# The first layer of a two-layer macaron block, laid out as one ordered stage with its mixtures beside the scan

## The chip, the core and the metric

The kernel runs on one core of a Trainium2 chip, in one launch. The metric is the device time in microseconds of that core, the median of several executions. The engines are PE (matmul, with PEld for its weight loads), DVE (vector), ACT (scalar functions), POOL (GpSimd) and SP, which only issues DMAs here. [...]

## The reference

The input x is 4 batches of 1024 tokens of 128 channels, all in fp32. Two layers follow, each a mixture, an attention-like part and the same mixture again. Only the first layer is touched:

```python
x = x + 0.5 * _L0_ffn_ref(_layernorm(x, axis=-1), ...)
x = x + _L0_attn_ref(_layernorm(x, axis=-1), ...)
x = x + 0.5 * _L0_ffn_ref(_layernorm(x, axis=-1), ...)
```

`_L0_ffn_ref` is a mixture of experts. A router gives 8 logits per token, the two best experts are kept and their softmax weights are scaled to sum to 1. Each expert is `w2 @ square(relu(w1 @ x))`. A shared expert, twice as wide, is added for every token. `_L0_attn_ref` is a selective state-space scan:

```python
u, res = jnp.split(x @ W_in, 2, axis=-1)
u = silu(conv of 3 taps over u, with W_conv)
dt, Bm, Cm = jnp.split(u @ W_x, [8, 24], axis=-1)
delta = jax.nn.softplus(dt @ W_dt + b_dt)
deltaA = jnp.exp(jnp.einsum('bld,dn->bldn', delta, A))
deltaB_u = jnp.einsum('bld,bln->bldn', delta * u, Bm)
# for each token: h = deltaA * h + deltaB_u;  y = sum over n of h * C
y = (y + u * D_param) * jax.nn.silu(res)
return y @ W_out
```

There are 256 inner channels (`DI` = 2 blocks of 128, index c) and 16 states (`NS`, index n).

## The kernel before

x stays in SBUF for the whole kernel, as `x_sb`, with 128 tokens on the partitions and 32 token tiles, 8 for each batch. The first layer runs as three stages: `moe0` over all batches, `s6` over all batches, `moe0` again. Instructions are put in order by a scheduler within and across these stages, following data dependences.

**moe0** (L152). For each batch: `layernorm_t` (L98) computes the statistics on DVE (L83, L84, and Newton steps L93 to L95 for the reciprocal root), normalizes (L108, DVE) and transposes on PE to channels on partitions, `xnt`. `route` (L120) makes logits and ranks them on DVE (L127 to L146). Then, for each half of 512 tokens and each expert, `hidden` makes hp by one 128x512 matmul (L181), Relu on ACT (L183), and squares on POOL (L185, `r*r`). Four 128x128 matmuls give `op` (L214, or L195 for the shared expert), and DVE adds `op` times the token's weight to `x_sb` (L218, four 128x128 operations an expert; L202 for the shared one). Three PSUM banks serve hp and three serve op.

**s6** (L231). For each batch: normalization; the input projection (L264), a copy, three DVE operations for the convolution (L273, L277) and Silu; `xd` by W_x (L291); softplus in pieces on DVE and ACT (L308 to L323), giving `delta` and `du`. Then the states, for each half of 512 tokens and each n: `sel` matmuls broadcast the row of B and the row of C over 128 partitions, `bp` (L334) and `cp` (L336), in PSUM; ACT copies cp to `c_sb` (L338). For each c, ACT makes `da` (L341), DVE makes `db = du * bp` (L345), with bp read from PSUM, and scans (L347). In the first half POOL copies the last column for the second half (L356). POOL multiplies by C (L358, `hm`), and PE adds hm into `yp` over n by an identity matmul (L359). After the 16 n, DVE adds `u * D`, multiplies by Silu(res) (L364, L372), PE projects (L376), and DVE adds to `x_sb` (L384).

Layer 1 starts with `moe1`, whose normalization and routing of all 4 batches take 1291 to 1342 us in the trace; the rest of layer 1 (head attention, mostly) follows and is not changed.

Of the kernel before, what the change touches and what calls it, by code (L numbers as in the profile page):

```python
# [20 lines left out]
I32 = mybir.dt.int32  # L21
# [55 lines left out]

def ln_stats(nc, sb, x, mv, rstd):

    n = x.shape[1]  # L80
    for i in range(n):
        st = sb.tile([P, nc.vector.BN_STATS_DIM], F32, name="ln_st", bufs=4)
        nc.vector.bn_stats(st, x[:, i, :])  # L83
        nc.vector.bn_aggr(mv[:, i, :], st)  # L84

    a = sb.tile([P, n], F32, name="ln_a")
    nc.vector.tensor_scalar(a, mv[:, :, 1], EPS, None, op0=ALU.add)
    q = sb.tile([P, n], F32, name="ln_q")
    nc.vector.tensor_scalar(
        rstd.bitcast(I32), a.bitcast(I32), -0.5, RSQRT, op0=ALU.mult, op1=ALU.add  # L90
    )
    for _ in range(3):
        nc.vector.scalar_tensor_tensor(q, rstd, -0.5, rstd, op0=ALU.mult, op1=ALU.mult)  # L93
        nc.vector.tensor_tensor(q, q, a, op=ALU.mult)
        nc.vector.scalar_tensor_tensor(rstd, q, 1.5, rstd, op0=ALU.add, op1=ALU.mult)  # L95
# [24 lines left out]
def route(nc, k, sb, ps, xnt, w_router, ex, mask):  # L120


    lg = ps.tile([P, GT, E], F32, name="lg", tag="tr")
    for i in range(GT):
        nc.tensor.matmul(lg[:, i, :], xnt[:, ts(i, P)], w_router, start=True, stop=True)
    mx = sb.tile([P, GT], F32, name="rt_mx")
    nc.vector.tensor_reduce(mx, lg, AX.X, ALU.max)  # L127
    d = sb.tile([P, GT, E], F32, name="rt_d")
    nc.vector.tensor_tensor(d, lg, mx[:, :, None].to_broadcast([P, GT, E]), op=ALU.subtract)
    nc.scalar.activation(ex, d, AF.Exp)  # L130
# [5 lines left out]
    eq = sb.tile([P, GT, E, E], F32, name="rt_eq")  # L136
    nc.vector.tensor_tensor(eq, other, own, op=ALU.is_equal)
    nc.vector.tensor_tensor(
        eq, eq, k.tri[:, None, :, :].to_broadcast([P, GT, E, E]), op=ALU.mult
    )  # L140
    above = sb.tile([P, GT, E, E], F32, name="rt_above")
# [6 lines left out]

def moe0(tc, k):  # L152


    nc = tc.nc
    with (
        tc.tile_pool(name="m0", bufs=2) as sb,
        tc.tile_pool(name="m0_tr", bufs=2, space=PSUM) as ps_tr,
        tc.tile_pool(name="m0_h", bufs=3, space=PSUM) as ps_h,
        tc.tile_pool(name="m0_o", bufs=3, space=PSUM) as ps_o,  # L160
    ):
        for g in range(B):
            xnt = sb.tile([P, L], F32, name="xnt")
            layernorm_t(nc, k, sb, ps_tr, g, xnt)
            ex = sb.tile([P, GT, E], F32, name="ex")
            mask = sb.tile([P, GT, E], F32, name="mask")
            route(nc, k, sb, ps_tr, xnt, k.wr0, ex, mask)

            w = sb.tile([P, GT, E], F32, name="w")
            nc.vector.tensor_tensor(w, ex, mask, op=ALU.mult)  # L170
            tot = sb.tile([P, GT], F32, name="tot")
            nc.vector.tensor_reduce(tot, w, AX.X, ALU.add)
            nc.vector.reciprocal(tot, tot)
            nc.vector.scalar_tensor_tensor(
                w, w, 0.5, tot[:, :, None].to_broadcast([P, GT, E]), op0=ALU.mult, op1=ALU.mult
            )

            def hidden(w1, cols):

                hp = ps_h.tile([P, 512], F32, name="hp")  # L180
                nc.tensor.matmul(hp, w1, xnt[:, cols], start=True, stop=True)  # L181
                r = sb.tile([P, 512], F32, name="r", bufs=3)
                nc.scalar.activation(r, hp, AF.Relu)  # L183
                h = sb.tile([P, 512], F32, name="h", bufs=4)
                nc.gpsimd.tensor_tensor(h, r, r, op=ALU.mult)  # L185
                return h

            for half in range(2):
                cols = ts(half, 512)
                t0 = g * GT + half * 4  # L190
                hs = [hidden(k.ws1[:, ts(f, P)], cols) for f in range(FS)]
                op = ps_o.tile([P, 4, C], F32, name="op")
                for i in range(4):
                    for f in range(FS):
                        nc.tensor.matmul(  # L195
                            op[:, i, :],
                            hs[f][:, ts(i, P)],
                            k.ws2[:, f, :],
                            start=(f == 0),
                            stop=(f == FS - 1),  # L200
                        )
                nc.vector.scalar_tensor_tensor(  # L202
                    k.x_sb[:, t0 : t0 + 4, :],
                    op,
                    0.5,
                    k.x_sb[:, t0 : t0 + 4, :],
                    op0=ALU.mult,
                    op1=ALU.add,
                )
                for e in range(E):  # L210
                    h = hidden(k.w1_0[:, e, :], cols)
                    op = ps_o.tile([P, 4, C], F32, name="op")
                    for i in range(4):
                        nc.tensor.matmul(  # L214
                            op[:, i, :], h[:, ts(i, P)], k.w2_0[:, e, :], start=True, stop=True
                        )
                    for i in range(4):
                        nc.vector.scalar_tensor_tensor(  # L218
                            k.x_sb[:, t0 + i, :],
                            op[:, i, :],  # L220
                            w[:, half * 4 + i, e : e + 1],
                            k.x_sb[:, t0 + i, :],
                            op0=ALU.mult,
                            op1=ALU.add,
                        )
# [5 lines left out]
def s6(tc, k):  # L231

    nc = tc.nc
    HL = 512
    with (
        tc.tile_pool(name="s6_c", bufs=1) as cst,
        tc.tile_pool(name="s6_b", bufs=2) as sb,
        tc.tile_pool(name="s6_w", bufs=3) as wk,
        tc.tile_pool(name="s6_tr", bufs=2, space=PSUM) as ps_tr,
        tc.tile_pool(name="s6_bc", bufs=2, space=PSUM) as ps_bc,  # L240
        tc.tile_pool(name="s6_y", bufs=1, space=PSUM) as ps_y,
    ):

        NR = DTR + 2 * NS
        sel = cst.tile([NR, 2 * NS, P], F32, name="sel")
        nc.vector.tensor_copy(sel, k.ident[0:NR, DTR:NR, None].to_broadcast([NR, 2 * NS, P]))
# [4 lines left out]
        for b in range(B):  # L251
            xnt = sb.tile([P, L], F32, name="xnt", bufs=1)
            layernorm_t(nc, k, sb, ps_tr, b, xnt)


            u = sb.tile([P, DI, L], F32, name="u")
            res = sb.tile([P, DI, L], F32, name="res")
            for c in range(2 * DI):
                if c < DI:
                    up = sb.tile([P, L + 2], F32, name="up", bufs=1)  # L260
                    nc.gpsimd.memset(up[:, 0:2], 0.0)
                for half in range(2):
                    pin = ps_tr.tile([P, HL], F32, name="pin", tag="tr")
                    nc.tensor.matmul(  # L264
                        pin, k.w_in[:, ts(c, P)], xnt[:, ts(half, HL)], start=True, stop=True
                    )
                    if c < DI:
                        nc.scalar.copy(up[:, 2 + half * HL : 2 + (half + 1) * HL], pin)
                    else:
                        nc.scalar.activation(res[:, c - DI, ts(half, HL)], pin, AF.Silu)  # L270
                if c < DI:
                    cv = sb.tile([P, L], F32, name="cv", bufs=1)
                    nc.vector.tensor_scalar(  # L273
                        cv, up[:, 0:L], k.w_conv[:, c, 0:1], None, op0=ALU.mult
                    )
                    for j in (1, 2):
                        nc.vector.scalar_tensor_tensor(  # L277
                            cv,
                            up[:, j : j + L],
                            k.w_conv[:, c, j : j + 1],  # L280
                            cv,
                            op0=ALU.mult,
                            op1=ALU.add,
                        )
                    nc.scalar.activation(u[:, c, :], cv, AF.Silu)

            xd = sb.tile([NR, L], F32, name="xd")
            for half in range(2):
                pxd = ps_tr.tile([NR, HL], F32, name="pxd", tag="tr")
                for c in range(DI):  # L290
                    nc.tensor.matmul(  # L291
                        pxd,
                        k.w_x[:, c, :],
                        u[:, c, ts(half, HL)],
                        start=(c == 0),
                        stop=(c == DI - 1),
                    )
                nc.scalar.copy(xd[:, ts(half, HL)], pxd)

# [862 lines left out]
```

## Time and profile before

| | us |
|---|---|
| runs shown, median | 8650.8 |
| runs shown, range | 8642.8 to 8652.7 |
| profiled execution, its time | 8645.8 |
| profiled execution, span of the trace | 8644.0 |
| ... first mixtures, 0 to 197 | 197 |
| ... scans of 4 batches with their preparation, 197 to 1108 | 911 |
| ... second mixtures, 1108 to 1291 | 183 |
| ... layer 1, 1291 to the end | 7353 |

The span is the time between the first and the last instruction in the trace. A line of a group names the kernel's line, the engine, the operation, what it writes and reads, and how often. PE's granted clock is given as a share of full speed.

The page's rows of busy tenths, 40 slices of 216 us each, show the first layer as the first six:

```profile
DVE  6766676777777777777777777777777777777773
ACT  2333324999999999999999999999999999999993
POOL 3554440000000000000000000000000000000000
PEclk9777797999999999999999999999999999999996
```

POOL works in the first layer alone. From the seventh slice on ACT is full: that is layer 1.

### The profile page before, as it was taken

The page shows a single profiled execution, that of the slowest core. Times are in us where ns is not written, and L with a number is a line of the kernel's source. Part 1 is how long each engine was busy: PE and PEld are TensorE (multiplying, and loading weights), DVE is VectorE, ACT ScalarE, POOL GpSimd, SP SyncE. Part 2 cuts the span into 40 slices and gives each one's busy share as a digit, 9 for nine tenths or more (in the row PEclk, how much of TensorE's full clock was granted, in tenths as well). Part 3 has the DMA queues.
Part 4 walks back from the last instruction along what each step waited for, and adds up shares of the span by engine and source line. Part 5 has one row for each costly group of instructions (what it writes and reads, how often), then busy time and mean ns, then how long its engine had stood idle before and what let it go on. Part 6 is the DMA issues. An engine that isn't in the chain of part 4 may idle for free. (4 is left out here: it accounts for less than half of the span.)

```text
span 8644.0 us, 174023 instructions
## 1 busy us (share of the span) xinstructions
PE 7278.9 (84%) x76602; PEld 3189.2 (37%) x76602; DVE 6580.4 (76%) x14818; ACT 7447.6 (86%) x1746; POOL 621.7 (7%) x642
## 2 busy tenths in 40 slices
PE   8888886888888888888888988888888888888885
PEld 5222253333333333333333433333334333333333
DVE  6766676777777777777777777777777777777773
ACT  2333324999999999999999999999999999999993
POOL 3554440000000000000000000000000000000000
PEclk9777797999999999999999999999999999999996
DMA  0000000000000000000000000000000000000000
GB/s 19 0 0 0 0 6 4 2 1 2 1 1 2 1 1 2 2 1 1 2 1 1 1 1 1 2 1 2 1 1 1 1 1 1 1 1 2 1 1 16
DMA packets 14660, 20.06 MB, mean 2 GB/s; under 512 B 3242, under 2 KB 12978, under 8 KB 13876
## 3 DMA queue, kind: packets, MB, share of 16 engines
q8 instruction: 611, 10.01, 0.5%
q1 hardware_dynamic: 9572, 6.01, 0.2%
q10 hardware_dynamic: 4304, 2.62, 0.1%
q14 instruction: 173, 1.42, 0.1%
HBM read 6.53 MB, written 2.10 MB: 1 GB/s over the span
## 5 line engine op out<-in xcount | busy, mean ns | idle before, releaser
L870 ACT ACTIVATE p_w<-xs,cc 128x7936 f32<-128x7936 f32 x1024 | 6971.4, 6898 | 92.3 <-PE o L880 73.9
L880 PE MATMUL o<-p_w,vt 128*9 128x256 f32 x63488 | 3829.5, 387 | 700.7 <-ACT p_w L870 695.2
L880 PEld LDWEIGHTS o<-p_w,vt 128*9 128x9 f32 x63488 | 1792.2, 92 | 2590.9 <-ACT p_w L870 1065.2
L789 DVE SCALAR_TENSOR_TENSOR x_p<-x_p,x_r 128x256 f32<-128x256 f32 x3072 | 1306.3, 425 | 105.4
L888 DVE COPY os<-o 128x256 f32<-128x256 f32 x1024 | 431.9, 422 | 580.4 <-PE o L880 579.5
L765 DVE COPY xs<-s 128x1024 f32<-128x1024 f32 x512 | 626.5, 1224 | 203.6 <-PE s L729 202.2
L743 DVE TENSOR_REDUCE nm<-s 128x1 f32<-128x1024 f32 x512 | 625.6, 1222 | 200.0 <-PE s L729 199.7
L880 PE MATMUL o<-p_w,vtop 128*9 128x256 f32 x2048 | 626.0, 388 | 9.8 <-DVE vtop L803 9.8
L906 PE MATMUL pt<-ident,os 128*128 128x128 f32 x2048 | 455.0, 304 | 168.7 <-DVE os L888 162.7
L729 PE MATMUL s<-kp,qp 32*128 32x512 f32 x2048 | 587.0, 650 | 0.7 <-DVE nm L743 0.7
L729 PE MATMUL s<-qp,kp 32*128 32x512 f32 x2048 | 583.1, 646 | 0.0
L906 PEld LDWEIGHTS pt<-ident,os 128*128 128x128 f32 x2048 | 208.2, 142 | 926.5 <-DVE os L888 789.0
L790 DVE SCALAR_TENSOR_TENSOR p_w<-x_p,x_e 128x256 f32<-128x256 f32 x1024 | 435.8, 426 | 109.4 <-DVE x_p L789 3.2
L359 PE MATMUL yp<-hm,ident 128*128 128x512 f32 x512 | 387.7, 878 | 105.5 <-POOL hm L358 103.9
L699 POOL COPY wp_q<-c_wq 128x32 f32<-128x32 f32 x32 | 6.9, 215 | 6151.4 <-PE pq L708 6151.4
L341 ACT ACTIVATE da<-delta,neg_a 128x512 f32<-128x512 f32 x256 | 182.7, 721 | 305.2 <-DVE hst L347 304.7
L787 DVE SCALAR_TENSOR_TENSOR x_p<-x_r 128x256 f32<-128x256 f32 x1024 | 429.1, 419 | 0.1
L781 DVE TENSOR_TENSOR x_r<-x_r,x_p 128x256 f32<-128x256 f32 x1024 | 428.5, 419 | 0.0
L358 POOL TENSOR_TENSOR hm<-hst,c_sb 128x512 f32<-128x512 f32 x256 | 369.9, 1457 | 172.6 <-ACT c_sb L338 119.7
L774 DVE TENSOR_SCALAR x_r<-xs,cc 128x256 f32<-128x256 f32 x1024 | 353.1, 345 | 1.0
L778 DVE TENSOR_SCALAR x_e<-x_p 128x256 int32<-128x256 f32 x1024 | 301.6, 295 | 35.0
L776 DVE TENSOR_SCALAR x_p<-x_r 128x256 f32<-128x256 f32 x1024 | 301.5, 294 | 35.0
(189 smaller groups left out, 4816.6 us busy)
## 6 DMA issues: line engine op xcount, KB each, us to landing
x_sb<-in_L_attn_x_dram ACTq DMA_DIRECT2D x4, 512.0 KB
c_w<-in_L_ffn_w_dram SPq DMA_DIRECT2D x4, 512.0 KB
out_dram<-x_sb SPq DMA_DIRECT2D x4, 512.0 KB
c_w<-in_L_ffn_w_stack_dram SPq DMA_DIRECT2D x1, 512.0 KB
c_w<-in_L_ffn_w_stack_dram ACTq DMA_DIRECT2D x1, 512.0 KB
c_ws<-in_L_ffn_ws_dram SPq DMA_DIRECT2D x2, 128.0 KB
c_w_in<-in_L_attn_W_in_dram SPq DMA_DIRECT2D x1, 256.0 KB
c_w_out<-in_L_attn_W_out_dram SPq DMA_DIRECT2D x1, 128.0 KB
```

The source lines that it names most:

```text
L359: nc.tensor.matmul(yp[c], k.ident, hm, start=(n == 0), stop=(n == NS - 1))
L729: nc.tensor.matmul(s[:, ts(half, 512)], a[row, ts(i, P)], c[row, ts(half, 512)], start=True, stop=True,)
L743: nc.vector.tensor_reduce(nm[:, i, 0:1], score(j, qp[n], i, kp[n]), AX.X, ALU.max, negate=True)
L765: nc.vector.tensor_copy(xs[u][:, i, :], score(j, kp[n], i, qp[n]))
L781: nc.vector.tensor_tensor(r, r, p, op=ALU.subtract)
L787: nc.vector.scalar_tensor_tensor(p, r, EXP2[4], r, op0=ALU.add, op1=ALU.mult)
L789: nc.vector.scalar_tensor_tensor(p, p, c, r, op0=ALU.add, op1=ALU.mult)
L790: nc.vector.scalar_tensor_tensor(p_w[g][:, 0, 0:SOFT], p, EXP2[0], e.bitcast(F32), op0=ALU.add, op1=ALU.mult,)
L870: nc.scalar.activation(p_w[g].rearrange("p a b -> p (a b)")[:, SOFT:], xs[u].rearrange("p a b -> p (a b)")[:, SOFT:], AF.Exp, scale=cc[:, ...
L880: nc.tensor.matmul(o[32 * r : 32 * r + D + 1, 0:QW], vtop[u] if soft else vts[b % 2][:, i, h, :], p_w[g][:, i, ts(r, QW)], start=(i == 0), ...
L888: nc.vector.tensor_copy(os, o[:, 0:QW])
L906: nc.tensor.transpose(pt[:, wl % 2 * 2 + c, :], os[:, ts(c, P)], k.ident)
```

## The change

`moe0` and `s6` are replaced by one function, `layer0`, whose instructions keep the order in which they are written, on all five queues. The pieces are generators, which are drawn in turn. The order:

- `route_rows(0)`, `route_rows(1)`, both halves of `experts(0)`, `prepare(0)`, `softplus(0)`.
- For each batch b: 18 steps of `states(b)`. After each step up to three pieces (two from step 10 on) of `beside(b)` are issued, and, once the batch's first mixture is through, one piece of `prepare(b + 1)`. `beside(b)` holds the first mixture of batch b + 1 and, from b = 1 on, the second mixture of batch b - 1. For the last batch only the latter.
- Then `close(b)` and `softplus(b + 1)` in turn, with two pieces of what is left of `beside(b)` after each, then the rest.
- At the end the second mixture of the last batch.

What is computed otherwise than before:

- The states run over 1024 columns at once, so that the scan needs no carried column (L356 goes). Rows of B and C are written to DRAM once a batch, and each n is read back into all 128 partitions by DMA, as `bc` (1 MB). `du` is thus multiplied by a tile in SBUF. POOL's product is written over the scan's result.
- The mixture's weights go into the square: the root of each token's weight (by an exponential of half the logit, and the reciprocal root of the sum) is written to DRAM and read back over 128 partitions as `m_w`; POOL multiplies Relu's result by it, ACT squares, and all ten products are added up in PSUM. DVE adds once for each half.
- The normalization's scaling goes from DVE to ACT. The convolution is put into the weights: `w_cv` is W_in times each tap, and three matmuls over shifted columns add up. W_conv is loaded over all partitions.
- PSUM: four banks for y, and one each for hp, op, the mixtures' transposes and the scan's small tiles.

The core of the diff:

```diff
+        tc.tile_pool(name="l0_y", bufs=1, space=PSUM) as ps_y,
+        tc.tile_pool(name="l0_t", bufs=1, space=PSUM) as ps_t,
+        tc.tile_pool(name="l0_r", bufs=1, space=PSUM) as ps_r,
+        tc.tile_pool(name="l0_h", bufs=1, space=PSUM) as ps_h,
+        tc.tile_pool(name="l0_o", bufs=1, space=PSUM) as ps_o,
+        tc.manual_schedule(engines=engines),
     ):
         neg_a = cst.tile([P, DI, NS], F32, name="neg_a")
         nc.scalar.activation(neg_a, k.a_log, AF.Exp)
         nc.vector.tensor_scalar(neg_a, neg_a, -1.0, None, op0=ALU.mult)
...
+        def route_rows(m):
+
+            m_x[m] = mb.tile([P, L], F32, name="m_x")
+            yield from normed(mb, ps_r, m % B, m_x[m])
+            lg = ps_r.tile([P, GT, E], F32, name="lg", tag="tr")
...
+            best_two(nc, mb, lg, d, mask, k.tri)
+
+            ex = mb.tile([P, GT, E], F32, name="ex")
+            nc.scalar.activation(ex, d, AF.Exp, scale=0.5)
+            yield
...
+                nc.sync.dma_start(out=m_rows[m][:, ts(half, HL)], in_=row)
+            yield
...
+        def experts(m, half, after):
...
+            for i in range(n + 2):
+                if i == 1:
+                    weights(m, half, 1)
+                if i == 7 and after:
+                    weights(*after, 0)
+                if i >= 2:
+                    j = i - 2
...
+                        nc.tensor.matmul(
+                            op[:, a, :],
+                            h[j][:, ts(a, P)],
+                            w2,
...
+                if i < n:
...
+                    nc.tensor.matmul(hp, w1, m_x[m][:, ts(half, HL)], start=True, stop=True)
+                    r[i] = mb.tile([P, HL], F32, name="r", bufs=3)
+                    nc.scalar.activation(
+                        r[i], hp, AF.Relu, scale=ROOT if i < FS else 1.0
+                    )
+                if 1 <= i <= n:
+                    j = i - 1
+                    if j >= FS:
+                        e = j - FS
+                        nc.gpsimd.tensor_tensor(
+                            r[j], r[j], m_w[m, half, e // 4][:, e % 4, :], op=ALU.mult
+                        )
+                    h[j] = mb.tile([P, HL], F32, name="h", bufs=3)
+                    nc.scalar.activation(h[j], r[j], AF.Square)
+                yield
+            nc.vector.tensor_tensor(
+                k.x_sb[:, t0 : t0 + 4, :], k.x_sb[:, t0 : t0 + 4, :], op, op=ALU.add
+            )
...
+        def states(b):
...
+            def rows(n):
+                bc[n] = sb.tile([P, 2, L], F32, name="bc", bufs=3)
+                nc.sync.dma_start(
+                    out=bc[n],
+                    in_=x_rows[b]
+                    .rearrange("(two n) l -> n two l", two=2)[n]
+                    .partition_broadcast(P),
+                )
+
+            def decay(n):
+                for c in range(DI):
+                    da[n, c] = sb.tile([P, L], F32, name="da", bufs=3)
+                    nc.scalar.activation(
+                        da[n, c], delta[b][:, c, :], AF.Exp, scale=neg_a[:, c, n : n + 1]
+                    )
+
+            rows(0)
+            rows(1)
+            decay(0)
+            for s in range(NS + 2):
+                if s + 2 < NS:
+                    rows(s + 2)
+                if s + 1 < NS:
+                    decay(s + 1)
+                if s < NS:
+                    for c in range(DI):
+                        hs[s, c] = sb.tile([P, L], F32, name="hs", bufs=6)
+                        nc.vector.tensor_tensor(
+                            hs[s, c], du[b][:, c, :], bc[s][:, 0, :], op=ALU.mult
+                        )
+                        nc.vector.tensor_tensor_scan(
+                            hs[s, c], da[s, c], hs[s, c], 0.0, op0=ALU.mult, op1=ALU.add
+                        )
+                if 1 <= s <= NS:
+                    for c in range(DI):
+                        t = hs[s - 1, c]
+                        nc.gpsimd.tensor_tensor(t, t, bc[s - 1][:, 1, :], op=ALU.mult)
+                if s >= 2:
+                    for c in range(DI):
+                        for half in range(2):
+                            nc.tensor.matmul(
+                                y[b][c][half],
+                                k.ident,
+                                hs[s - 2, c][:, ts(half, HL)],
...
+                yield
...
+        run(route_rows(0))
+        weights(0, 0, 0)
+        run(route_rows(1), experts(0, 0, (0, 1)), experts(0, 1, (1, 0)))
+        run(prepare(0), softplus(0))
+        for b in range(B):
+            mix = beside(b)
+            ready = b == B - 1
+            ahead = iter(())
+            for s, _ in enumerate(states(b)):
+                for _ in range(3 if s < 10 else 2):
+                    if next(mix, None) == "ready":
+                        ready = True
+                        ahead = prepare(b + 1)
+                if ready:
+                    next(ahead, None)
...
+            run(ahead)
+            for _ in both(close(b), softplus(b + 1) if b + 1 < B else ()):
+                next(mix, None)
+                next(mix, None)
+            run(mix)
+        run(route_rows(2 * B - 1))
+        weights(2 * B - 1, 0, 0)
+        run(experts(2 * B - 1, 0, (2 * B - 1, 1)), experts(2 * B - 1, 1, None))
```

`prepare`, `softplus` and `close` hold the work of `s6` before and after the states: normalization, three shifted matmuls and Silu for each c and half, xd and the DMA of its rows; delta and du as before; then Silu(res), the sum with `u * D`, the output projection and the addition to `x_sb`.

## The prediction

> **What bounds the kernel now.** I read the page first. The change touches only layer 0, so I then cut the trace into layer 0's stages with the windows view. Columns: stretch, its length, busy us of PE, PEld, DVE, ACT and POOL with instruction counts, granted PE clock, DMA share, GB/s.
>
> ```profile
> 0.00:197.00 197.00, 168.44 (x903) 116.34 (x903) 131.58 (x510) 54.89 (x95) 83.81 (x96) 0.98 0.08 21
> 461.00:650.00 189.00, 160.68 (x258) 50.62 (x258) 138.64 (x141) 66.90 (x98) 109.97 (x96) 0.74 0.00 0
> 650.00:690.00 40.00, 31.18 (x71) 11.65 (x70) 17.88 (x25) 19.37 (x27) 0.20 (x2) 0.79 0.00 0
> 1108.00:1291.00 183.00, 167.94 (x911) 116.31 (x910) 126.27 (x459) 53.16 (x92) 82.20 (x80) 0.96 0.00 1
> 1291.00:1342.00 51.00, 22.27 (x98) 20.11 (x98) 38.55 (x197) 5.72 (x12) 0.00 (x0) 0.54 0.06 21
> ```
>
> Layer 0 ends at 1291 us: mixtures 0-197 and 1108-1291 (about 48 a mixture, PE-bound), and between them per batch some 189 us of states and 40 us of preparation. The rest, 7353 us, is layer 1; of it only the first mixture's opening, 1291-1342, can shift against layer 0.
>
> In the states no engine is full. The answers on single lines (count, ns min/median/max) and the timeline (start, us) say why:
>
> ```profile
> L358 POOL TENSOR_TENSOR hm<-hst,c_sb x256: 1252/1268/2244, 239.0 to 1103.8; 128x512 f32<-128x512 f32 x128
> L356 POOL COPY last<-hst x128: 174/373/1142, 238.5 to 1015.6; 128x1 f32<-128x1 f32 x128
> L345 DVE TENSOR_TENSOR db<-du,bp x256: 656/682/690, 235.2 to 1098.8; 128x512 f32<-128x512 f32 x128
> L319 DVE SCALAR_TENSOR_TENSOR sp_z<-sp_w,sp_z x8: 1224/1764/2306, 222.2 to 922.4; 128x1024 f32<-128x1024 f32 x8
> ...
> 306.82 2.50 POOL L358 TENSOR_TENSOR hm<-hst,c_sb 128x512 f32<-128x512 f32 x2
> 308.11 3.40 DVE L347 TENSOR_TENSOR_SCAN hst<-da,db 128x512 f32<-128x512 f32 x2
> 310.46 1.03 POOL L356 COPY last<-hst 128x1 f32<-128x1 f32 x1 [1.14 <-DVE hst L347]
> ...
> 239.02 1.26 POOL L358 TENSOR_TENSOR hm<-hst,c_sb 128x512 f32<-128x512 f32 x1
> 239.05 2.31 DVE L319 SCALAR_TENSOR_TENSOR sp_z<-sp_w,sp_z 128x1024 f32<-128x1024 f32 x1
> ```
>
> A one-column copy takes 0.17 us alone and 1.03 beside a scan; products and scans last twice as long when they meet. They take turns. The second operation ends about 1.06 us (product 128x512) or 1.08 us (scan 128x512) after the first; L319, no scan but a DVE operation with two SBUF inputs, ends at 241.36, 1.08 us after the product's end at 240.28. L345, whose second input is in PSUM, never waits (maximum 690).
>
> **What the Trainium skill says.** "SBUF — State Buffer", section "Who interferes with whom": a DVE instruction with two SBUF inputs contends with a GpSimd instruction that reads SBUF, the second blocking until the first ends; one with at most one SBUF input, outside the 2-port modes, does not. The trace agrees (1030 against 174 ns; L345 flat). "ScalarE: Activation LUTs", "What ACT_TABLE_LOAD costs": a switch of table set costs a load of about 1283 ns; the trace has 1283. "TensorE: Matmul & The Clock Gate", Part 1: an idle array falls to half clock; the trace grants 0.98 in the mixtures, 0.74 in the states, 0.54 at 1291-1342.
>
> **The change, part by part.**
>
> *States.* Gone: the matmuls bp and cp (256 each), the copies c_sb, the copies last, and DVE's wait for bp (170 us). But `du*bc` (L439 of the changed kernel) now reads two SBUF tiles, so it joins the turns. Held time per batch, 32 pairs (n, c) at 1024 wide: du*bc 1.08 (as L319), scan 2 x 1.08 = 2.16, product 2 x 1.06 = 2.12: 5.36 x 32 = 171. Before, per 16 n with both halves: 64 x (1.08 + 1.06) = 137 plus the copies' 32 x 0.17 = 5, 142 held in some 174 us of steady loop, 82% used. Width saves nothing, because held time goes by elements.
>
> *Mixtures beside states.* Six of eight run there, in 12 halves of 8 POOL products (r*m_w). They now share the turns: a 128x512 product holds 1.06. The order of POOL's instructions puts them, by batch, at 16, 26, 26 and 16: 17, 28, 28, 17 us. Their and the preparation's DVE work also stands in DVE's queue between scans: a normalization 5.5 (1360.41 to 1365.86 in the trace), a ranking 3.9 plus about 2.9 of small operations, adds 0.7. Two normalizations and one ranking in batches 0 to 2, one each in batch 3: 20, 20, 20, 14 (less what runs in POOL's turns). Sums: 208, 219, 219, 202 = 848. I take the turns 93% used, since the loads of B and C come by DMA well ahead (1 MB per step of some 12 us; the first 100 us moved 40 GB/s at a DMA share of 0.14, so 285 GB/s at full share, 3.7 us per MB as an estimate): 910. Bounds: 100% 848, today's 82% 1034.
>
> *An exposed mixture.* In the order, step i stands as op(i-2), hp(i) on PE and Relu(i), Square(i-1) on ACT, with one hp bank. So hp (0.95) → Relu (0.60) → Square (0.6) → four op (1.06) → next hp: 3.2 us, at a clock of about 0.85 (PE 60% used) 3.6. Twenty steps so and four of about 1.7: 79 us, against some 48 before.
>
> *Opening.* DVE's queue begins with neg_a (needs a_log, the tenth SP load) and w_cv: about 15 us where the trace starts at 5.3. Then route_rows(0): normalization 5.7, eight ACT normalizations with two transposes and copies 4.9, lg 1.8, ranking 3.9, weights 2.9, transposes out 3.2: 22. route_rows(1) stands ahead of the first mixture on every engine: 20 more, to 57. Mixture 79. prepare(0): 10.6, then four convolutions of three matmuls plus Silu 13.6, xd 4.9. softplus(0): 2 x 12 = 25 (trace: L311 to L323 with two table loads). States start at 191 (range 175 to 215) with one mixture done; before, at 235 with four.
>
> *Between batches.* Last product and y matmuls 6, then close and softplus share one PSUM bank and ACT's order, with two table loads more than before: 32. That is 38 after batch 0 (before: 46.7 from L345 to L345). After batch 1, 15 mixture steps are left over, at about 3.3 us: 68. After batch 2, 9: 52. After batch 3: 19. Together 177.
>
> *End.* route_rows(7) 22, with layer 1's normalizations of batches 0 to 2 put into the same DVE queue, 8; mixture 79; rows' DMAs 3: 112. In return some 20 of the 51 us at 1291-1342 are already done.
>
> Accumulating ten products in PSUM and dropping L218 (512 x 0.34 = 174 us of DVE) is worth nothing by itself: L218 ran under PE's mixtures. Roots and Square likewise: they swap a POOL square for an ACT one.
>
> Sum: 191 + 910 + 177 + 112 = 1390 against 1291, less 20: +79. On the profiled span, 8644 + 79 = 8723; that execution took 8645.8, and the median shown is 5 above. **Forecast 8725.**
>
> **Rivals.**
> 1. *The turns stay as loosely used as today* (82%): a weight product or decay arrives late because ACT's queue holds it behind a decay that waits for a scan. States 1034: 8725 + 124 = 8849. For it: L341 waited 305 us for scans before. Against: no PSUM round trip, three buffers of da, six of hs.
> 2. *Faster: du\*bc does not take turns.* Its 128 x 1.08 = 138 us leave the sum; 710 held at 93% = 763: 8725 - 147 = 8578. Against: L319. It decides once at least 79 of the 138 are hidden; short of that the layer is not faster.
> 3. *The broadcast loads bind.* No trace shows one row of HBM read into 128 partitions; 64 such loads for B and C and 24 for the weights, 1 MB each, stand in the states. They decide once one takes over 910 / 88 = 10.3 us (about 100 GB/s); at 12 us, 1056: 8725 + 146 = 8871.
> 4. *No change*, if losses at both ends and the gain between the batches cancel (opening 180, states 860, boundaries 165 and end 106 make 1311, less 20 the old 1291).
>
> **How the numbers follow.** Forecast 0.48, rival 1 0.22, rival 2 0.16, rival 3 0.06, rival 4 0.08. The forecast's own case spans 8660 to 8790 (opening ±15, states 860 to 960, boundaries ±25). The range goes up to rival 1 and down far enough to hold the no-change case: 8620 to 8880; rival 2 and the tail of rival 3 stay out. About 0.2% (17 us) is what a measurement of this kernel can tell from no change: faster 0.17, same 0.08, slower 0.75.
>
> **What would show it.** Right: in the states the products (L448) and scans (L442) show maxima near twice their minima, as does L439 (minimum 1.22, often above 2); POOL and DVE together are busy for nearly the whole stage; POOL and DVE wait for each other rather than for DMA; states begin near 190; a lone mixture takes near 79 with ACT waiting for PE each step. Wrong: L439 flat at 1.22 (rival 2), DVE waiting for bc (rival 3), layer 0 under 1291 in spite of long L439.

## The result and the profile after

| | before | after |
|---|---|---|
| median, us | 8649.9 | 8708.9 |
| range, 4 runs each | 8642.8 to 8652.7 | 8707.5 to 8715.9 |
| span of the profiled execution | 8644.0 | 8714.1 |
| layer 0 ends (last add into `x_sb`) | 1291.0 | 1366.3 |
| attention of layer 1 begins (first 128x7936 activation) | 1416.5 | 1482.4 |

The changed kernel is slower by a factor of 1.0073, 95% interval 1.0061 to 1.0086. The forecast was 8725 in a range of 8620 to 8880. The spans lie 70 us apart, the medians 59; both executions are single ones, so some 10 us between these two figures mean nothing.

First the page's rows of busy tenths of the changed kernel, 40 slices of 218 us:

```profile
DVE  3886684777777777777777777777777777777773
ACT  3333323999999999999999999999999999999992
POOL 1564560000000000000000000000000000000000
PEclk8777787999999999999999999999999999999996
```

POOL now has more work in the middle of the first layer and less at its start, and DVE stands at six to eight tenths there. From the eighth slice on the rows are as before: that is layer 1. So the layer is cut into stages again. This is the windows view of the changed kernel: stretch, length, busy us of PE, PEld, DVE, ACT and POOL with instruction counts, granted PE clock, DMA share, GB/s.

```profile
0.00:196.00 196.00, 93.47 (x314) 47.15 (x314) 44.90 (x149) 60.24 (x100) 21.60 (x33) 0.91 0.23 71
196.00:401.00 205.00, 134.38 (x386) 67.61 (x386) 188.06 (x145) 72.61 (x101) 132.85 (x47) 0.79 0.25 82
401.00:452.00 51.00, 30.50 (x63) 12.34 (x62) 20.22 (x23) 19.12 (x21) 2.34 (x1) 0.64 0.26 85
452.00:662.00 210.00, 140.05 (x446) 74.55 (x446) 191.57 (x146) 80.68 (x117) 148.80 (x53) 0.80 0.27 90
662.00:760.00 98.00, 66.80 (x235) 33.47 (x234) 33.68 (x76) 41.44 (x61) 17.27 (x12) 0.81 0.20 66
760.00:969.00 209.00, 139.63 (x446) 74.68 (x446) 195.53 (x146) 80.92 (x117) 150.90 (x53) 0.80 0.28 91
969.00:1049.00 80.00, 53.43 (x201) 29.49 (x200) 21.69 (x25) 33.08 (x46) 17.34 (x12) 0.88 0.16 54
1271.00:1366.00 95.00, 52.91 (x240) 31.55 (x240) 22.39 (x145) 30.17 (x55) 20.29 (x16) 0.85 0.15 45
```

In the states (second, fourth and sixth line) DVE is busy for over nine tenths of the stretch; the time in which an operation waits for its turn counts as busy here. In the opening, the boundaries between batches and the end no engine is: the opening has 93 us of PE and 45 of DVE in 196, and the boundary from 662 to 760 has no engine above 67 of 98. What the change won lies in the first kind of stretch, what it lost in the second.

The answers on single lines of the changed kernel (count, ns minimum/median/maximum) show the turns that VectorE and GpSimd take:

```profile
L439 DVE TENSOR_TENSOR hs<-du,bc x128: 1192/1638/3312, 195.7 to 1245.2; 128x1024 f32<-128x1024 f32 x128
...
L442 DVE TENSOR_TENSOR_SCAN hs<-da,hs x128: 2291/4242/4324, 197.0 to 1246.5; 128x1024 f32<-128x1024 f32 x128
...
L448 POOL TENSOR_TENSOR hs<-hs,bc x128: 2330/3154/4356, 199.4 to 1250.9; 128x1024 f32<-128x1024 f32 x128
```

The median scan takes 4.24 us where a scan alone takes 2.29. The multiplication of `du` by the row of B, flat at 682 ns (128x512) before, now reaches 3312: it has joined the turns.

### The profile page after: what moved, and what is told of

It is laid out like the page before. It is cut to its first block, busy times and chain, and to the rows that moved or that the text cites. A ratio compares the mean times of both kernels' runs of the same rounds, so it can differ in the third digit from the quotient of the medians.

```text
span 8714.1 us, 172103 instructions
## 1 busy us (share of the span) xinstructions
PE 7034.7 (81%) x76218; PEld 3154.5 (36%) x76218; DVE 6596.7 (76%) x14024; ACT 7479.3 (86%) x1767; POOL 673.1 (8%) x348
## 5 line engine op out<-in xcount | busy, mean ns | idle before, releaser
L442 DVE TENSOR_TENSOR_SCAN hs<-da,hs 128x1024 f32<-128x1024 f32 x128 | 451.4, 3527 | 13.0 <-DVE hs L439 0.5
L448 POOL TENSOR_TENSOR hs<-hs,bc 128x1024 f32<-128x1024 f32 x128 | 409.5, 3214 | 335.6 <-DVE hs L442 256.7
L317 ACT ACTIVATE r<-hp 128x512 f32<-128x512 f32 x160 | 95.4, 596 | 361.1 <-PE hp L315 361.0
```

Of the source, the lines that this page charges most:

```text
L442: nc.vector.tensor_tensor_scan(hs[s, c], da[s, c], hs[s, c], 0.0, op0=ALU.mult, op1=ALU.add)
```

## The experiments

Layer 1 branches on counts that come out of layer 0's result, so where a kernel leaves out part of the computation I compare the end of layer 0 and its stages, not the whole time. "States" is from the first scan of a batch to its last, summed over the four batches; "boundaries" is from there to the next batch's first scan, for the three gaps. The changed kernel has 821 and 233 by this measure (52, 100 and 81). The first four kernels below ran once each, so differences of some 10 us in their times mean nothing.

**Does the multiplication by B cost turns?** In the kernel before, B's row was copied to SBUF, so that the multiplication reads two SBUF tiles:

```diff
+                    b_sb = wk.tile([P, HL], F32, name="b_sb")
+                    nc.scalar.copy(b_sb, bp)
-                        nc.vector.tensor_tensor(db, du[:, c, hc], bp, op=ALU.mult)
+                        nc.vector.tensor_tensor(db, du[:, c, hc], b_sb, op=ALU.mult)
```

> The kernel before, with one part of the change alone: ACT copies the row of B into SBUF, so that db = du * B reads two SBUF tiles. Turns theory: db joins the turns of scan and product. Held time per batch rises from 142 us by 64 x 0.54 = 35 us to 177, so the loop of about 174 us per batch grows by 12 us (turns then fully used) to 42 us (used at 82% as now): 8700 to 8820 us in all, about 8770; db's longest goes from 690 ns to about 1.6 us. Rival (the states wait for PE's round trip of bp, not for the turns): db stays at 690 ns at most and the time stays within 20 us of 8650.

Measured, as expected: 8759.1 us beside 8643.9 for the kernel before, one run each; layer 0 ends at 1401.2, that is 110 later. The multiplication's durations went from 656/682/690 to 660/693/1774, with a mean of 1047. The copies on ScalarE are in this figure as well, so it isn't the price of the turns alone.

The other way round, in the changed kernel the second input was put into PSUM, as a constant:

```diff
-                            hs[s, c], du[b][:, c, :], bc[s][:, 0, :], op=ALU.mult
+                            hs[s, c].rearrange("p (t l) -> p t l", t=2),
+                            du[b][:, c, :].rearrange("p (t l) -> p t l", t=2),
+                            bz[:, None, :].to_broadcast([P, 2, HL]),
+                            op=ALU.mult,
```

> The changed kernel with du multiplied by a constant tile in PSUM in place of B's row in SBUF (the row of B is loaded and not used; the two pools of small PSUM tiles become one to make room). Turns theory: the multiplication leaves the turns and is flat at 1.2 us; a clean step falls from 10.9 to 10.7 - 2.16 = 8.6 us, all states by at most 128 x 1.08 = 138 us, with mixtures beside them perhaps half of it: 8570 to 8660. Rival (du * bc costs only its own time on DVE): no change in the step, 8709 within 20 us.

The answer on the line of that multiplication:

```profile
L443 DVE TENSOR_TENSOR hs<-du,bz x128: 1187/1194/1223, 195.7 to 1174.8; 128x1024 f32<-128x1024 f32 x128
```

It is flat again, at the same shape and count. The states fell from 821 to 745 us and layer 0 ended at 1296.2, 70 us sooner; the whole time was 8640.8. A step of the states without any mixture beside it fell from 10.9 to 9.4 us, where I had expected 8.6: a scan and a product that never overlap take 2.29 + 2.33 = 4.62, twice that is 9.2.

This is rival 2 of the prediction made real, and it is worth about half of the 138 us that the prediction gave it: the multiplication holds the turns, but part of what it gives back, the scans and products take for themselves. Without its turns the changed layer still ends 5 us behind the 1291.0 of the layer before: they are about as large as the loss, and to be rid of them would not have made the change a gain.

**How closely are the turns used?** The product by C and the products with the routes' weights were left out, one at a time:

```diff
-                        nc.gpsimd.tensor_tensor(t, t, bc[s - 1][:, 1, :], op=ALU.mult)
+                        pass
```

> The changed kernel without POOL's product by C: y sums the states themselves. Turns theory: where no mixture runs beside the states (the last steps of the first batch), a step falls from the 10.9 us measured to DVE's own 2 x (1.15 + 2.2) = 6.7 us, scans are flat at 2.3 us; steps with mixtures are then set by the mixtures' chain, about 13 us. States of a batch 206 to about 165, the whole about 8709 - 160 = 8550. Rival (the order of ACT and PE sets the step): the step stays near 10.9 and the whole within 30 us of 8709.

Layer 0 ended at 1197.8, 168 us sooner, with the states at 645, or 161 a batch where 165 was expected. A step without mixture took 7.0 us: DVE's own 2 x (1.19 + 2.29) = 6.96 and nothing else. The whole time (8465.9) fell by 243; 74 us of this lie after layer 1's attention (94 us from its last 128x7936 activation to the end of the span, against 168), which is not a stage that the edit touches.

```diff
-                    if j >= FS:
-                        e = j - FS
-                        nc.gpsimd.tensor_tensor(
-                            r[j], r[j], m_w[m, half, e // 4][:, e % 4, :], op=ALU.mult
-                        )
```

> The changed kernel without POOL's product of Relu's result and the token's weight; ACT squares Relu's result directly. Turns theory: 96 of the 128 products stand in the states or their boundaries and hold 1.06 us each, so up to 100 us go: 8610 to 8650. A lone mixture keeps its 3.28 us per step, since POOL's product is not on its chain. Rival (the chain of hp, Relu, Square and op sets mixture steps beside the states too): under 30 us go, 8680 or more.

The whole time, 8892.8, misses the expectation and can't be compared: layer 1 ran experts that it skips otherwise. Layer 0 ended at 1294.8, 71.5 us sooner, and the states took 753. By the starts in the trace of the changed kernel, 78 of the 128 weight products lie in the states (16, 23, 23 and 16). They thus cost 67 us there, 0.86 each against 1.06 in the prediction. Of the 60 steps from one state's first multiplication to the next's, 37 are now 10.9 to 11.0 us long; the longest, 17 to 21 us, hold a route's pieces or the normalization of the next preparation. The timeline of two pairs (start, us, engine, line) shows how a step is filled:

```profile
365.32 1.19 DVE L434 TENSOR_TENSOR hs<-du,bc 128x1024 f32<-128x1024 f32 x1
...
365.57 3.15 POOL L443 TENSOR_TENSOR hs<-hs,bc 128x1024 f32<-128x1024 f32 x1 [2.32 <-DVE hs L437]
...
366.62 4.25 DVE L437 TENSOR_TENSOR_SCAN hs<-da,hs 128x1024 f32<-128x1024 f32 x1
...
370.79 1.19 DVE L434 TENSOR_TENSOR hs<-du,bc 128x1024 f32<-128x1024 f32 x1
```

The multiplication runs first, to 366.51. The product, issued meanwhile, ends at 368.72, 2.21 later. The scan, issued when the multiplication is done, ends at 370.87, 2.15 after the product. From one multiplication to the next it is 5.47 us, against 5.36 of held time in the prediction: the turns are used to 98%. Note that the multiplication shows its own 1.19 us here, though it takes part in the turns; the operation that comes second carries the wait.

**What makes the boundaries long?** The mixture was paced faster, so that no step of it would be left over for a boundary (15 steps after the second batch, 9 after the third, by the order of the program):

```diff
-                for _ in range(3 if s < 10 else 2):
+                for _ in range(4 if s < 10 else 3):
```

> The changed kernel with the mixture paced four steps to each of the first ten steps of the states and three after that, so that none of its 72 steps is left for the boundary between two batches. Theory (the two long boundaries, 98 and 80 us, hold some dozen left-over mixture steps each, which stand in ACT's and PE's order ahead of the work that the boundary needs): these boundaries fall to about 50 to 55 us like the first one (51 us), 60 to 70 us less; the states take up to 13 us more for the products that come into them (12 x 1.06); about 8655 us (8635 to 8680). Rival (a left-over step costs the same beside the states as in the boundary): within 15 us of 8709.

Measured: 8750.2 us, slower than the changed kernel, ratio to the kernel before 1.0122 (1.0107 to 1.0138). The theory was half right. The boundaries fell to 44, 68 and 49 us, 72 less, as expected. But the states grew from 821 to 933, by 112 instead of 13. The timeline of VectorE and then of GpSimd in the first batch's states:

```profile
217.06 3.17 DVE L442 TENSOR_TENSOR_SCAN hs<-da,hs 128x1024 f32<-128x1024 f32 x1
230.56 2.71 DVE L439 TENSOR_TENSOR hs<-du,bc 128x1024 f32<-128x1024 f32 x1 [10.33 <-PE y L452]
```

```profile
223.02 1.27 POOL L324 TENSOR_TENSOR r<-r,m_w 128x512 f32<-128x512 f32 x1 [1.73 <-ACT r L317]
226.29 1.26 POOL L324 TENSOR_TENSOR r<-r,m_w 128x512 f32<-128x512 f32 x1 [2.00 <-issue]
227.52 4.67 POOL L448 TENSOR_TENSOR hs<-hs,bc 128x1024 f32<-128x1024 f32 x2
```

GpSimd's order puts the weight products of four mixture steps ahead of the states' products by C. They come 3.27 us apart, since a mixture step is a chain of that length (below); four take 13.1 us, and a step of the states only 10.9. So the products by C come late, the buffers of `hs` stay taken, and VectorE stands still for 10.3 us. Three mixture steps, 9.8 us, fit. How much of the 112 us this is, the kernel of all three edits shows below.

**What binds a lone mixture step, its one buffer or its order?** This is the chain in the changed kernel's opening:

```profile
82.18 1.16 PE L305 MATMUL op<-c_w,h 128*128 128x128 f32 x8 [1.26 <-ACT h L328]
...
83.17 1.02 PE L315 MATMUL hp<-m_x,c_w 128*128 128x512 f32 x2
84.29 0.60 ACT L317 ACTIVATE r<-hp 128x512 f32<-128x512 f32 x1 [2.17 <-PE hp L315]
84.79 0.62 ACT L328 ACTIVATE h<-r 128x512 f32<-128x512 f32 x1
...
85.46 1.16 PE L305 MATMUL op<-c_w,h 128*128 128x128 f32 x8 [1.26 <-ACT h L328]
...
86.45 1.02 PE L315 MATMUL hp<-m_x,c_w 128*128 128x512 f32 x2
```

`op`, `hp`, Relu and Square follow each other, and both engines wait in every step: 85.46 - 82.18 = 3.28 us. The buffer is not what holds `hp` back: Relu, which reads it, ends at 84.89, and the next `hp` starts only at 86.45. In between stands `op` of the step before, ahead of it in TensorE's order and waiting for Square. The edit changes both, order and buffer: `hp` is issued ahead of `op`, and gets a second buffer so that it can run ahead of Relu:

```diff
-        tc.tile_pool(name="l0_h", bufs=1, space=PSUM) as ps_h,
+        tc.tile_pool(name="l0_h", bufs=2, space=PSUM) as ps_h,
...
+                if i < n:
+                    w1 = k.ws1[:, ts(i, P)] if i < FS else k.w1_0[:, i - FS, :]
+                    hp = ps_h.tile([P, HL], F32, name="hp")
+                    nc.tensor.matmul(hp, w1, m_x[m][:, ts(half, HL)], start=True, stop=True)
                 if i >= 2:
```

> The changed kernel with a second buffer for a mixture step's first matmul (the two small PSUM pools share one tag to make room), and that matmul issued one step further ahead, before the output matmul of two steps earlier. Theory (a lone mixture step is a chain of matmul, Relu, Square and matmul with one buffer, 3.28 us a step): the lone step falls to about 2.1 us, what PE alone needs; two exposed mixtures get some 22 us shorter each, and the left-over steps in the long boundaries shrink too: about 8650 us (8620 to 8670). Rival (the step is not bound by that buffer but by its engines' order): the lone step stays at 3.2 to 3.3 us and the time within 10 us of 8709.

Measured: 8629.0 us, ratio to the kernel before 0.9977 (0.9968 to 0.9985): this alone makes the kernel faster than it was before the change. The same stage of the mixture:

```profile
74.92 1.05 PE L308 MATMUL op<-c_w,h 128*128 128x128 f32 x8
...
75.81 1.02 PE L303 MATMUL hp<-m_x,c_w 128*128 128x512 f32 x2
...
76.67 1.05 PE L308 MATMUL op<-c_w,h 128*128 128x128 f32 x8
```

A step now takes 76.67 - 74.92 = 1.75 us, and PE's matmuls follow each other without a wait. The opening is 30 us shorter, the three boundaries 27, what follows the last states 27; the states stay at 822. The theory had the gain right, but put it down to the buffer; by the times above it was the order, and so the rival's cause, that bound the step. Whether the new order needs the second buffer was not tried.

**The opening.** The constants `neg_a` and `w_cv` were made after the first mixture, and the second batch's route was put between the steps of that mixture:

```diff
-        run(route_rows(1), experts(0, 0, (0, 1)), experts(0, 1, (1, 0)))
+        run(both(first(), route_rows(1)))
+        neg_a = cst.tile([P, DI, NS], F32, name="neg_a")
```

> The changed kernel with only the opening changed: the constants that the states need are made after the first mixture instead of before it, and the second batch's route is put between the steps of the first batch's lone mixture instead of ahead of it. Theory (the opening is a sum of stages on nearly idle engines): DVE's first useful work comes some 12 us sooner and the 20 us of the route are hidden beside the mixture's chain: layer 0 ends 30 us sooner, about 8680 us (8665 to 8695). Rival (the route's matmuls and copies stand in the same order as the mixture's chain and lengthen it by as much): 8697 or more.

Measured: 8682.2 us; the states begin at 170.5 instead of 197.0, and layer 0 ends 30 us sooner. That is 26.5 of the 32 us that the two parts were to bring: the lone mixture, from its first matmul to its last addition, takes 81 us with the route's pieces between its steps, against 72 without.

**Together.** All three edits at once:

> The paced mixture, the earlier first matmul and the new opening together. If the three parts are separate costs of the changed kernel they add: about 8565 us (8540 to 8600), below both kernels. If the pace and the earlier matmul pay for the same left-over steps, 8600 to 8630. If the exposed stages are not what costs the time, 8690 or more.

Measured: 8632.5 us, ratio 0.9985 (0.9978 to 0.9992), outside all three of my ranges, just above the second. The first range had counted on a gain from the pace. With what the edits did alone, 41 us more for the pace, 80 and 27 less for the others, the sum is 8644 us, so the measured time is 11 us below plain addition, and the pace is the loss among the three. Without the pace:

> The earlier first matmul and the new opening together, at the pace of the changed kernel (3 and 2 mixture steps to a step of the states), that is the kernel of all three parts without its faster pace. Theory (the two are separate costs, and the faster pace costs more in the states than it saves in the boundaries, whatever the length of a lone step): 8629 less the 27 us of the opening, about 8602 us (8590 to 8615), 30 us below the kernel with the pace. Rival (with the shorter lone step the faster pace is no loss, and the two gains overlap in the opening): 8625 or more.

Measured: 8610.5 us, ratio 0.9958 (0.9944 to 0.9971), as the theory said. Between these two kernels only the pace differs: with it the boundaries are 157 us instead of 209, but the states 895 instead of 821. So the pace costs 74 us in the states even where a lone mixture step is 1.75 us and four of them, 7.0 us, would fit into a step of the states, against 112 with the chain of 3.28. The long chain thus accounts for some 38 of the 112 us, the smaller part. Part of the rest is in the route. In the kernel of all three edits four of its six pieces fall into one step of the states, and VectorE's timeline there reads:

```profile
177.85 3.30 DVE L426 TENSOR_TENSOR hs<-du,bc 128x1024 f32<-128x1024 f32 x1
...
203.07 0.17 DVE L210 SCALAR_TENSOR_TENSOR ln_shift<-ln_mv,ln_rstd 128x8 f32<-128x8 f32 x1
213.03 0.22 DVE L129 TENSOR_REDUCE rt_mx<-lg 128x8 f32<-128x64 f32 x1 [9.79 <-PE lg L240]
...
217.38 1.22 DVE L426 TENSOR_TENSOR hs<-du,bc 128x1024 f32<-128x1024 f32 x1
```

The first and the last line are the first multiplications of this step and of the next. Between the two lines of the route lie eight normalizations on ScalarE and their transposes and logits on TensorE. VectorE waits 9.8 us for them, with the next multiplication and scan behind in its order; this step took 39.5 us instead of 10.9. So the pieces were kept apart, with no mixture step after one in the same step of the states:

```diff
+                    if told == "slow":
+                        break
```

> As the kernel of the earlier first matmul and the new opening, and besides no mixture step follows a piece of a route in the same step of the states, so that the six pieces of a route lie in six steps instead of two. Theory (the two long steps at a route, 16 and 20 us against 10.9, hold VectorE waiting in its order for the route's own chain over ScalarE and TensorE): the five routes save some 5 us each, the left-over mixture steps cost up to 15 us in the boundaries: 5 to 20 us below the kernel without it. Rival (these steps are long by VectorE's own work for the route, some 12 us of it): no gain in the states, and the boundaries grow: 5 to 20 us above it.

Measured: 8675.7 us, ratio 1.0035 (1.0021 to 1.0049). The states fell to 781, by 40 us, where five routes at 5 us each had been to save 25. Not all of it is the routes': 19 weight products left the states (61 lie there instead of 80), and at the 0.86 us found above they are worth some 16 us. That leaves some 23 us, near the 5 a route of the theory; this split is an estimate. But the steps put off came back in the boundaries, 304 us instead of 209, far more than the 15 allowed, and the kernel is 65 us slower than without this edit, above the rival's range too. Last, one piece of a route after each two steps of the mixture that runs at the time, and four steps of either kind to a step of the states in the two middle batches:

```diff
+        def threaded(a, m):
+            extra = route_rows(m)
+            for i, _ in enumerate(a):
+                yield
+                if i % 2:
+                    next(extra, None)
+                    yield
+            yield from extra
...
-                for _ in range(3 if s < 10 else 2):
+                for _ in range((3 if s < 10 else 2) + (0 < b < B - 1)):
```

> The earlier first matmul and the new opening, and besides the pieces of a route put between the steps of the mixture that runs at that time (one piece after each two), and four mixture steps to a step of the states (three from the eleventh on) for the second and third batch, which then have none left over. Theory (route pieces in a row hold VectorE for their own chain; left-over steps cost about 2 us each in a boundary; a mixture step of 1.75 us beside the states costs only its product on POOL, 1.06 us, where no more than four come to a step): the boundaries after the second and third batch fall from 87 and 69 us to about 65 and 50, the states of these batches stay at 205 to 220 us: 8565 us (8545 to 8595). Rival (four steps of any kind to a step of the states hold it up, as the faster pace did, 239 us for the second batch's states): 8610 to 8640.

Measured: 8596.3 us, ratio 0.9945 (0.9931 to 0.9958), between the two expectations. The boundaries did what was expected:

```profile
403.00:632.00 229.00, 163.82 (x564) 93.03 (x564) 195.91 (x197) 102.49 (x152) 140.02 (x58) 0.84 0.27 88
632.00:691.00 59.00, 40.17 (x116) 20.11 (x116) 21.52 (x24) 25.43 (x30) 10.49 (x7) 0.74 0.27 92
...
911.00:961.00 50.00, 30.39 (x76) 13.06 (x74) 21.03 (x24) 20.95 (x23) 6.37 (x3) 0.72 0.19 66
```

They take 59 and 50 us. The states of the middle batches take 229 and 219 where 205 to 220 was expected; DVE is busy for 196 of the 229, so some 33 us are still idle. Layer 0 ends at 1249.6, against 1267.7 with the two edits alone and 1291.0 before the change. The intervals of these two kernels overlap, so that the last 14 us between their medians aren't shown by the times.

## Why the prediction was right, and where it was not

The direction and the reason held: the turns stay the limit of the states, and the first layer pays at both ends for two exposed mixtures. That the total came out within 16 us is partly luck: the states were set 84 us too high and the boundaries 72 too low. By the windows of the changed kernel:

| stage | predicted | measured |
|---|---|---|
| opening | 191 | 196 |
| states | 910 | 826 |
| between batches | 177 | 249 |
| end | 112 | 95 |
| sum | 1390 | 1366 |
| of layer 1's opening already done | 20 | 11 |

The sum's last step has a small slip: the forecast adds 79 to the 8645.8 of the profiled execution. Added to the median of 8650.8 it would be 8730.

- *States.* The step "I take the turns 93% used" failed. In the clean stretch of the kernel without weight products, a multiplication, a scan and a product take 5.47 us where their held time was put at 5.36, so nearly nothing is lost; rival 1 (82%) is out. That held time goes by elements was right: 2.21 and 2.15 us at 1024 columns against 1.06 and 1.08 at 512. The stage came out even under the 848 of full use. Two of that sum's terms were too high: of the 84 weight products put into the states 78 lie there, at 0.86 us and not 1.06; and without them the states take 753 us, 53 more than 128 x 5.47 = 700, where I had put 74 of VectorE's other work, part of which runs in GpSimd's turns, as the prediction allowed.
- *du\*bc takes turns.* Right. It reached 3.3 us in the changed kernel and was flat at 1.19 with a PSUM input, and the states were then 76 us shorter. This agrees with the Trainium skill, "SBUF — State Buffer", section "Who interferes with whom", by which a DVE instruction with two SBUF inputs contends with a GpSimd instruction that reads SBUF. The 138 us that rival 2 set for it were nearly twice the price. One of my signs was badly chosen: a flat multiplication was to speak for rival 2, but in the kernel without weight products it is flat as a first comer, and the turns go on.
- *Between batches.* This is the term that was mis-sized: 38, 68, 52 and 19 against 51, 98, 80 and 20. The left-over steps were taken to lie partly beside the boundary's own work: 30 us for 15 steps, 14 for 9. They cost 47 and 29, 3.1 and 3.2 us a step, nearly all of their 3.28. VectorE's longest wait in the changed kernel between 662 and 760 us (engine, what waited, for what: total, times, longest) is for ScalarE:

```profile
DVE u L485 <- ACT res L476: 43.5, 4, 14.9
```

`close` stands in ScalarE's and TensorE's order behind pieces of route, preparation and mixture, each of them a chain between the same engines. The other 13 us are in each boundary between two batches, the first too. The trace shows a reason for most of them: the last pieces of the preparation, two copies with their matmuls, still lie behind the end of the states (to 412 us after the first batch, whose states end at 401).
- *An exposed mixture.* The chain was named rightly, though its one bank isn't a link of it; 3.28 us a step instead of 3.6. The clock of 0.85 in that term came from no trace; the windows show 0.91 in the opening and 0.85 in the end. The two lone mixtures take 72 and 70 us instead of 79, and what stands ahead of the last one 26 instead of 33, so the end is 95 instead of 112.
- *Opening.* 196 against 191, but its parts were off both ways: the mixture's first matmul starts at 67 us instead of 57, the mixture takes 7 us less, and the rest 57 us where 54 was put. Making `neg_a` and `w_cv` late and hiding the route brought 27 us.
- *Loads of B and C.* No wait of VectorE for `bc` shows in the states, so rival 3 is out.
- *Layer 1.* From layer 0's end to the branch on the first count of routes it takes 40 us instead of 51. The normalizations put into the end save 11 us, not 20.

So 75 us are lost in layer 0, 11 come back, and the attention of layer 1 begins 66 us later; the other 2 us lie between that branch and the attention.

The middle of the layer grew by 164 us, from 911 to 826 + 249 = 1075, when it took in six of the eight mixtures; the ends, which they left, shrank only by 89, from 197 + 183 = 380 to 196 + 95 = 291. Two things are each as large as the difference: the turns of `du*bc` (layer 0 ends 70 us sooner without them) and the exposed pieces, the chain of a lone mixture step and the opening, whose two edits take 98 us off the median and leave a kernel faster than the one before. Both were shown by runs. Why the middle batches of the best kernel still lose some 20 us, and whether a different order of `close` and `softplus` would shorten the boundaries of 50 us, was not tried.

## What to carry to other kernels

When work is moved beside a stage that has room on its engines, add up not only its busy time but its chains: how long a piece takes from its first operation to its last, and what stands behind it in each engine's order. Here late weight products held up the products of the states, and a route of which four pieces fell into one step made that step 39.5 us long instead of 10.9. Count what is left over, and price it at the full length of its chain. Issuing the first link of a chain ahead of the last link of an earlier step, here with a second buffer, brought 80 us, more than the whole rearrangement had lost. Where two engines take turns, read the sum of their held times from a clean stretch, and look at the operation that comes second.

## What the runs showed that was not expected

- Packing is not monotone: at three mixture steps to a step of the states a weight product costs 0.86 us, while a pace of four costs the stage 112 us more (74 with the short chain).
- A scan and a product with nothing between them take 4.7 us a pair (9.4 for two), about as long as both alone (4.62); with the multiplication taking turns as well, the three take 5.47, though alone they are 1.19 + 2.29 + 2.33 = 5.81. So about 0.1 us is gained at each change of turn among the three; why the pair gains nothing stays open.
